# Leaf slots with dealt blocks, in place of every leaf's units, in the tree networks of a two-layer Perceiver kernel

## The chip, the cores and the metric

The kernel runs on one core of a Trainium2 chip. The metric is device time in microseconds of that core, as the median of the runs shown. The profile is one further execution of the same program, with its own time.

## The reference, cut to what matters

An input x of 16 batches of 64 tokens (1024 tokens in all, 256 features, float32) passes through two layers, each with a cross attention over 16 x 1601 memory rows, a second mixing step and a feed-forward part, each added to x. The change is in the last part of the second layer: three fast-feedforward networks f = q, k, v. Each is a binary tree of depth 4 with 15 nodes and 16 leaves, and each leaf is a small two-layer network of width 64. A token walks down the tree, and only its own leaf counts:

```python
def fff(x, node_w, node_b, w1, b1, w2, b2):          # for each of q, k, v
    cur = 0                                          # per token
    for _ in range(4):
        score = (x * node_w[cur]).sum(-1) + node_b[cur]
        cur = 2 * cur + 1 + (score >= 0)
    leaf = cur - 15
    sel = one_hot(leaf, 16)
    hidden = relu(einsum('nd,ldh->lnh', x, w1) + b1[:, None, :]) * sel.T[:, :, None]
    return einsum('lnh,lho->no', hidden, w2) + sel @ b2
# x = x + softmax(q k^T / 16) v, within each batch of 64 tokens, on x after a layer norm
```

The weights of one network are 1 MB for `w1` (256 x 1024: leaf l owns the columns 64 l to 64 l + 63), 1 MB for `w2` (1024 x 256) and 16 KB for `b2`.

## The kernel before, in words

**Order of the program.** First comes layer 0: cross attention with a top-32 choice, a retention step, self-attention, and a mixture of experts. The experts' tokens go through DRAM: an indirect DMA on POOL scatters rows to `disp` (L1025), SP reads them back (L1045), and another indirect DMA gathers the results (L1153). Then comes layer 1: the cross attention over the memory in 128 units (16 batches, 4 parts of the memory, 2 groups of heads), then for each half of the tokens (h = 0 and 1, 512 tokens each) the generator `after_attention(h)`: output projection, random features, a last layer norm, and the walk down the three trees. The networks come last.

**What sets the order.** In these stages the instructions of PE, DVE and ACT run in the order in which the code emits them (`tc.manual_schedule`), and Python generators written as steps are interleaved by hand. `LATE_STEPS` says how many steps of `after_attention(0)` run beside each of the last 16 attention units; what is left of it, and `after_attention(1)`, run beside the networks, one step at a time. The queues of SP and POOL are ordered by the framework's planner. Each engine and each queue is in order, so an instruction that waits holds up all behind it. A DMA issued by SP takes one of eight semaphores in turn, and it waits until the DMA that had that semaphore before it has landed.

**Steps of `after_attention(h)` that matter here.** SP reads the heads' results of half h from the DRAM tile `by_head` (L1397). `norm_steps` takes statistics on DVE and an inverse root and the scaling on POOL. `turned_half` turns tokens to features with PE transposes. `by_pairs` and `rates` are matmuls. The node scores are 8 small matmuls (L1482), and three rounds of five small DVE operations (L1505 to L1512) walk the trees; `cur` then holds the leaf of each token and network.

**The networks.** For each half h and network f there are three pieces of work. `hidden(i)` multiplies all 512 tokens by the whole `w1`: 8 blocks of 128 hidden units, two matmuls with 512 columns each (L1796), and ACT adds the bias and the relu (L1803). `leaves(i)` spreads the leaf numbers of the tokens over all partitions with PE (L1776). `masked(i, m)` sets the hidden units of other leaves to zero on DVE (L1785). `given(i)` multiplies by the whole `w2` (L1818 for q and k, L1830 for v) and adds `b2` of the leaf with a matmul of 16 partitions (L1823, L1836). All 16 leaves are thus computed for every token. `attended(h)` then does the 64 x 64 softmax attention (L1854 to L1883), and the rows go out by SP (L1888).

## Time and profile before

| what | us |
|---|---|
| median of 3 runs (lowest, highest) | 1532.55 (1529.1, 1533.01) |
| the profiled execution: its time | 1526.84 |
| the profiled execution: its span | 1525.1 |
| from the first hidden matmul of the networks to the end of the span | 231.8 (1293.3 to 1525.1) |
| PE busy in the windows 1293 to 1411 and 1411 to 1525.1 | 111.78 of 118, 106.78 of 114.1 |

The span runs from the first to the last instruction of the profiled execution. A float32 matmul appears as two records (a transpose as one), so 64 records are 32 matmuls. The mean duration of a group is that of one record with its latency; the pace of back-to-back matmuls is read from the chain or the timeline, where a matmul with 512 columns takes 0.86 us.

### The profile page before, as it was taken

What the parts mean: (1) busy time and instruction counts of PE and PEld (TensorE: products, weight loads), DVE (VectorE), ACT (ScalarE), POOL (GpSimd) and SP (SyncE); (2) the same over time, 40 slices, a digit from 0 to 9 for tenths busy, and PEclk for the clock granted to TensorE, in tenths of its full rate; (3) what the DMA queues carried; (4) which work ended last, traced back from release to release, by engine and by line L of the source; (5) the groups of instructions that cost most, each with busy time, mean ns of one, the idle gap of its engine ahead of it and who ended that gap; (6) DMA issues with size and microseconds to landing.
All of it is one profiled execution on the core that took longest, in us unless ns stands there. A gap on an engine that the chain in (4) does not pass through costs nothing.

```text
span 1525.1 us, 28151 instructions
## 1 busy us (share of the span) xinstructions
PE 1460.4 (96%) x10994; PEld 996.7 (65%) x10994; DVE 998.8 (65%) x2135; ACT 786.2 (52%) x1979; POOL 321.9 (21%) x789
## 2 busy tenths in 40 slices
PE   7999888999988999999999999999999998989999
PEld 4666546677866777777777777777777765446445
DVE  2888848771159877877787787778776666523332
ACT  4666422351056666666666666666666555211221
POOL 2000017202032223132312312230331322321000
PEclk9999999999989999999999999999999999999999
DMA  9455042034821011011001101110110121000000
GB/s 327 141 173 172 2 135 72 1 111 145 263 78 44 3 45 46 4 46 45 22 28 45 46 3 46 45 46 3 45 44 4 45 85 31 16 0 0 0 14 14
DMA packets 76597, 92.86 MB, mean 61 GB/s; under 512 B 2584, under 2 KB 71760, under 8 KB 76336
## 3 DMA queue, kind: packets, MB, share of 16 engines
q1 hardware_dynamic: 72912, 82.82, 17.0%
q0 software_dynamic: 2400, 7.20, 1.9%
q8 instruction: 86, 1.41, 0.4%
q10 hardware_dynamic: 1152, 1.05, 0.2%
q14 instruction: 47, 0.39, 0.1%
HBM read 85.82 MB, written 5.24 MB: 60 GB/s over the span
## 4 chain that ended last, share of the span: by engine, by line
PE 87%; DVE 7%; DMA 2%; ACT 1%; issue 1%; POOL 1%; DVEq 0%; POOLq 0%; SPq 0%; ACTq 0%
PE ps_v L624 12%; PE ps_k L602 11%; PE pt L1565 9%; PE sc L1530 7%; PE po L1585 7%; PE ps_h L1796 5%; PE ps_o L1818 4%; PE pt L325 3%; PE sc L338 3%; PE ps_p L209 3%; DVE nmax L1543 3%; PE pu L410 3%; PE pt L581 3%; PE ps_h L1069 2%; PE ps_v L1830 2%; PE ps_y L1083 2%
## 5 line engine op out<-in xcount | busy, mean ns | idle before, releaser
L1551 ACT ACTIVATE a<-sc,nmax 128x384 f32<-128x384 f32 (+2 forms) x512 | 304.4, 600 | 162.4 <-DVE nmax L1543 162.4
L1543 DVE TENSOR_REDUCE nmax<-sc 128x1 f32<-128x384 f32 (+2 forms) x512 | 258.1, 566 | 96.1 <-PE sc L1530 96.0
L1565 PEld LDWEIGHTS pt<-ident,a 128*128 128x128 f32 (+1 forms) x1664 | 188.2, 141 | 47.0 <-issue 26.4
L1573 DVE COPY aT<-pt 128x512 f32<-128x512 f32 (+1 forms) x288 | 191.2, 685 | 34.3 <-PE pt L1565 26.1
L602 PE MATMUL ps_k<-mT,w_x 128*128 128x384 f32 (+2 forms) x512 | 205.2, 524 | 1.1 <-ACT mT L586 1.1
L624 PE MATMUL ps_v<-w_x,mT 128*128 128x256 f32 (+1 forms) x832 | 202.7, 383 | 2.9 <-ACT kT L610 1.0
L1565 PE MATMUL pt<-ident,a 128*128 128x128 f32 (+1 forms) x1664 | 203.3, 273 | 0.0
L624 PEld LDWEIGHTS ps_v<-w_x,mT 128*128 128x128 f32 (+1 forms) x832 | 146.4, 187 | 25.3 <-DVE aT L1573 5.1
L602 PEld LDWEIGHTS ps_k<-mT,w_x 128*128 128x128 f32 x512 | 87.1, 189 | 104.6 <-issue 72.1
L1530 PE MATMUL sc<-kT,qh 32*128 32x384 f32 (+2 forms) x1024 | 124.0, 547 | 0.0
L1585 PE MATMUL po<-aT,v 128*32 128x128 f32 (+1 forms) x3328 | 118.3, 277 | 6.0 <-DVE aT L1573 6.0
L586 ACT ACTIVATE mT<-pt,cols 128x384 f32<-128x384 f32 (+2 forms) x128 | 86.7, 683 | 66.1 <-PE pt L581 65.9
L568 POOL TENSOR_SCALAR memt<-memt,m_nmean,m_rstd 128x256 f32<-128x256 f32 (+1 forms) x208 | 111.8, 554 | 1.8
L1551 ACT ACTIVATION_READ_ACCUMULATOR a<-sc,nmax 128x1 f32 x512 | 105.9, 207 | 0.0
L1585 PEld LDWEIGHTS po<-aT,v 128*32 128x32 f32 (+1 forms) x3328 | 82.6, 110 | 31.6 <-issue 14.4
L610 ACT ACTIVATE kT<-ps_k,cols 128x384 f32<-128x384 f32 (+2 forms) x128 | 76.0, 594 | 39.6 <-PE ps_k L602 39.6
L632 DVE COPY v<-ps_v 128x512 f32<-128x512 f32 (+1 forms) x112 | 64.9, 580 | 35.3 <-PE po L1585 28.0
L562 DVE BATCH_NORM_STATS2 m_st<-memt 128x6 f32<-128x256 f32 (+1 forms) x208 | 82.9, 403 | 5.8 <-DMA memt<-in_mem_dram 5.5
L1570 ACT COPY aT<-pt 128x512 f32<-128x512 f32 x128 | 75.6, 591 | 0.7 <-PE pt L1565 0.7
L1785 DVE SCALAR_TENSOR_TENSOR hT<-leafb,memt,hT 128x512 f32<-128x512 f32 x48 | 35.2, 746 | 60.0 <-ACT hT L1803 60.0
L581 PE MATMUL pt<-ident,memt 128*128 128x128 f32 (+1 forms) x416 | 67.4, 276 | 3.8 <-ACT mT L586 3.3
L1803 ACT ACTIVATE hT<-ps_h,cols 128x512 f32<-128x512 f32 x48 | 33.0, 687 | 73.4 <-PE ps_h L1796 73.4
(365 smaller groups left out, 2019.9 us busy)
## 6 DMA issues: line engine op xcount, KB each, us to landing
memt<-in_mem_dram SPq DMA_DIRECT2D x32, 1536.0 KB
w<-in_moe_w_dram SPq DMA_DIRECT2D x16, 1024.0 KB
memt<-in_mem_dram SPq DMA_DIRECT2D x32, 65.0 KB
w_x<-in_w_x_dram POOLq DMA_DIRECT2D x2, 1024.0 KB, 10.5
mT<-in_fff_w_dram SPq DMA_DIRECT2D x2, 1024.0 KB
kT<-in_fff_w_dram SPq DMA_DIRECT2D x2, 1024.0 KB
rows<-in_rows_dram SPq DMA_DIRECT2D x1, 1430.5 KB
X<-in_x_dram SPq DMA_DIRECT2D x2, 512.0 KB
```

Source lines behind the costliest of these rows:

```text
L562: nc.vector.bn_stats(out=st[0:m, c, :], in_=mt[0:m, c, :])
L568: nc.gpsimd.tensor_scalar(mt[0:m, c, :], mt[0:m, c, :], nmean[0:m, c : c + 1], rstd[0:m, c : c + 1], ALU.add, ALU.mult,)
L581: nc.tensor.transpose(pt[:, j * P : j * P + chunk(c)], mt[0 : chunk(c), c, dc * P : (dc + 1) * P], ident[0 : chunk(c), 0 : chunk(c)],)
L586: nc.scalar.activation(mT[:, dc, c0 * P : c0 * P + n], pt[:, 0:n], AF.Identity, bias=col("L1_norm_b", dc), scale=col("L1_norm_w", dc),)
L602: nc.tensor.matmul(ps[:, 0:n], lhsT=wk[:, dc, oc * P : (oc + 1) * P], rhs=mT[:, dc, n0 : n0 + n], start=(dc == 0), stop=(dc == 1),)
L624: nc.tensor.matmul(ps[0 : chunk(c), j, :], lhsT=mT[:, dc, c * P : c * P + chunk(c)], rhs=wv[:, dc, :], start=(dc == 0), stop=(dc == 1),)
L1530: nc.tensor.matmul(scs[j][:, 0:n], lhsT=qh[rs, oc, b, :, :], rhs=kT[rs, oc, c0 * P : c0 * P + n], start=True, stop=True,)
L1543: nc.vector.reduce_max(out=nm, in_=sc[:, 0:n], axis=AX.X, negate=True)
L1551: nc.scalar.activation(aj[:, 0:n], sc[:, 0:n], AF.Exp, bias=nm, accum_out=tot[:, blk, part : part + 1])
L1565: nc.tensor.transpose(pt[0:m, j * P : (j + 1) * P], a[j][:, c * P : c * P + m], ident)
L1573: nc.vector.tensor_copy(aT[0:m, :], pt[0:m, :])
L1585: nc.tensor.matmul(po[32 * j : 32 * j + 32, :], lhsT=v[0:m, c0 + c, blk * 32 : (blk + 1) * 32], rhs=aTs[c][0:m, j * P : (j + 1) * P], star ...
```

## The change

Tokens are sorted to slots by leaf, so that each token meets only its own leaf's weights.

1. For each half and network there is a DRAM tile `slots_in` of 1536 rows: 16 leaves with 64 slots each, and 8 further blocks of 64 slots for leaves with more than 64 tokens. `zeros()` clears all six (1.5 MB each) from SP during the attention.
2. `placed(h, leaf, xn)`, at the end of `after_attention(h)`, computes the slot of every token (a count of earlier tokens of the same leaf with matmuls on PE, and 22 small DVE operations), which leaf each of the 8 further blocks is dealt to, and scatters the rows of `xn` with 12 indirect DMAs on POOL.
3. The networks of a half run as nine thirds `third(h, f, c)` of 512 slots. c = 0 and 1 are the leaves 0 to 7 and 8 to 15 with their weights in place; c = 2 is the eight dealt blocks. `fetch_third`, two thirds ahead, reads the slots from DRAM and the biases `b2`. For c = 2 SP loads eight leaf numbers to registers and issues 24 DMAs (8 blocks, each with a piece of `w1`, of `w2` and of `b2`) whose source address is the register.
4. A third is 8 transposes, 16 matmuls 128 x 64 x 64, relu, 8 matmuls 64 x 64 x 256, an addition to the biases on DVE, and a 512 KB store to `slots_out`. After c = 2 four indirect DMAs on POOL gather the tokens' rows back; q and k are then turned again with 8 transposes.
5. `LATE_STEPS` is changed so that all of `after_attention(0)`, `placed` included, runs within the attention; `pause` counts in `after_attention(1)` are raised; and the networks of half 0 run beside `after_attention(1)`, those of half 1 after it. `hidden`, `leaves`, `masked` and `given` are gone.

```diff
-LATE_STEPS = {0: 1, 2: 2, 3: 2, 4: 1, 5: 1, 6: 2, 8: 1, 9: 1, 10: 1, 11: 1, 12: 2, 14: 1, 15: 1}
+LATE_STEPS = {0: 3, 1: 2, 2: 1, 3: 3, 5: 1, 6: 2, 7: 3, 9: 1, 10: 2, 11: 3, 12: 1, 13: 2}
+    def zeros():
+        zero = spare_rows[:, 512:768]
+        nc.vector.memset(zero, 0.0)
+        for h in range(2):
+            for f in range(3):
+                nc.sync.dma_start(
+                    out=slots_in[h][f].rearrange("(n p) d -> p n d", p=P),
+                    in_=zero.unsqueeze(1).to_broadcast([P, NSLOT // P, D]))
...
+    def placed(h, leaf, xn):
...
+        for f in range(3):
+            sent = scattered[h, f] = []
+            for k in range(4):
+                sent.append(nc.gpsimd.indirect_dma_start(
+                    out=slots_in[h][f],
+                    out_offset=bass.IndirectOffsetOnAxis(
+                        ap=to_rows[h][:, 3 * k + f : 3 * k + f + 1], axis=0),
+                    in_=xn[:, k, :], in_offset=None).ins)
...
+        def fetch_third(h, f, c):
+            xs = arrived[h, f, c] = work.tile([P, 4, D], F32, name="xs", tag="xs", bufs=3)
+            read = nc.sync.dma_start(out=xs, in_=slots_in[h][f][c * 512 : (c + 1) * 512, :]...)
...
+            y = filled[h, f, c] = places[(h + 3 * f + c) % 4]
+            if c < 2:
+                biases = fff_b2[f].rearrange("(m s) o -> s m o", s=2)
+                for side in range(2):
+                    nc.sync.dma_start(out=y[side * 64 : (side + 1) * 64, :, :],
+                        in_=biases[side, c * 4 : (c + 1) * 4, :].partition_broadcast(64))
+                return
+            _, numbers = nc.values_load_multi_w_load_instructions(
+                over_leaf[h][0:1, f * 8 : (f + 1) * 8], engines=[mybir.EngineType.SP], ...)
...
+            at = (h + f) % 2
+            for i in range(8):
+                one = bass.ds(numbers[i], 1)
+                sl = slice(i % 2 * 64, (i % 2 + 1) * 64)
+                nc.sync.dma_start(out=dealt1[at][:, i, :]..., in_=first[:, :, one, :]...)
+                nc.sync.dma_start(out=dealt2[at][sl, i // 2, :], in_=second[one, :, :]...)
+                nc.sync.dma_start(out=y[sl, i // 2, :], in_=fff_b2[f][one, :].to_broadcast([64, D]))
...
+        def networks(h):
+            thirds = [(h, f, c) for f in range(3) for c in range(3)]
+            for i, (_, f, c) in enumerate(thirds):
+                if i + 2 < len(thirds):
+                    fetch_third(*thirds[i + 2])
+                yield from third(h, f, c)
+                if c == 2:
+                    back(h, f)
+                if c == 1 and f > 0:
+                    turned_back(h, f - 1)
+                    yield
+            yield from attended(h)
...
         with tc.manual_schedule(engines=order):
-            for step, _ in enumerate(networks()):
...
+            for c in range(2):
+                fetch_third(0, 0, c)
+            work_of = networks(0)
+            for _ in joining:
+                next(work_of)
...
+            for _ in after_attention(1):
+                next(work_of, None)
+            for c in range(2):
+                fetch_third(1, 0, c)
+            run(work_of)
+            run(networks(1))
```

The new function that does the work of one third, with what is left out marked:

```python
        def third(h, f, c):
            xs = arrived.pop((h, f, c))
            xsT = work.tile([P, 2, 512], F32, name="xsT", tag="xsT")
            for dc in range(2):
                ...                                   # 4 transposes, copied by ACT (dc 0) or DVE (dc 1)
            yield
            ps = ps_f.tile([P, 4, WIDTH], F32, name="ps_h", tag="mm")
            ...                                       # 16 matmuls: 64 slots x 64 units, two halves of 128 features
            hT = row(("L1_bq", "L1_bv")[(f + c) % 2]).rearrange("p (j t) -> p j t", j=4)
            ...                                       # bias and relu: ACT for c < 2, DVE and ACT for c = 2
            yield
            y = filled.pop((h, f, c))
            for j0 in (0, 2):
                ps = ps_f.tile([P, 2, D], F32, name="ps_y", tag="mm")
                ...                                   # 4 matmuls: 64 slots x 256 outputs, one leaf each
                part = y[:, j0 : j0 + 2, :]
                nc.vector.tensor_tensor(part, ps, part, ALU.add)
            nc.sync.dma_start(
                out=slots_out[h][f][c * 512 : (c + 1) * 512, :].rearrange("(m p) d -> p m d", p=P),
                in_=y,
            )
            yield
```

## The prediction

> **What bounds the kernel now.** I read the page's busy shares and chain first, then busy time by stage, then the groups of the last stage, and last the rows nearest to what the change adds.
>
> ```profile
> PE 1460.4 (96%) x10994; PEld 996.7 (65%) x10994; DVE 998.8 (65%) x2135; ACT 786.2 (52%) x1979; POOL 321.9 (21%) x789
> PE 87%; DVE 7%; DMA 2%; ACT 1%; issue 1%; POOL 1%; DVEq 0%; POOLq 0%; SPq 0%; ACTq 0%
> ```
>
> PE is busy 96% and carries 87% of the chain that ended last. By stage (span; then busy time of PE, PEld, DVE, ACT, POOL; granted clock, DMA share, GB/s):
>
> ```profile
> 1250.00:1293.00 43.00, 37.15 (x396) 25.44 (x400) 27.98 (x63) 23.43 (x73) 9.62 (x28) 1.00 0.13 37
> 1293.00:1411.00 118.00, 111.78 (x361) 58.77 (x356) 44.98 (x118) 25.24 (x40) 28.69 (x67) 0.99 0.02 6
> 1411.00:1525.10 114.10, 106.78 (x373) 56.31 (x372) 31.60 (x58) 22.89 (x37) 0.00 (x0) 1.00 0.03 10
> ```
>
> The networks (from 1293) are PE's alone, with idle DMA queues. In the end of the attention PE already loses 6 of 43 us. The nearest rows to the new work (timeline: start, duration, records, idle before; and rows by tile):
>
> ```profile
> 1444.45 1.20 PE L1854 MATMUL ps_s<-kT,qT 128*64 128x64 f32 x32
> 194.56 5.83 PE L410 MATMUL pu<-memt,aT 128*64 128x256 f32 x52
> 352.80 0.97 POOL L1025 DMA_INDIRECT disp<-y,to_row  x1 [0.30 <-issue]
> 355.47 0.92 SPq L1045 DMA_DIRECT2D dsp<-disp  x2
> 359.46 1.94 PE L191 MATMUL ps_t<-ident,dsp 128*128 128x128 f32 x8 [3.38 <-DMA dsp<-disp]
> 360.00:365.00 5.00, 5.00 (x23) 4.71 (x22) 1.38 (x2) 1.17 (x2) 0.00 (x0) 0.50 0.02 7
> DMA to landing us min/median/max: 2.7/2.8/3.3
> 64.14 0.37 SPq L241 DMA_DIRECT2D memt<-in_mem_dram  x1
> 64.55 0.78 SPq L244 DMA_DIRECT2D memt<-in_mem_dram  x1
> L1505 DVE TENSOR_TENSOR rows<-memt,rows 128x180 f32<-128x180 f32 x6 | 2.1, 345 | 0.2
> L1349 DVE BATCH_NORM_STATS2 c_st<-X 128x6 f32<-128x256 f32 x8 | 3.3, 407 | 0.0
> ```
>
> From the last scatter of `disp` to its first use on PE is 359.46 - 352.80 = 6.7 us. SP issues a DMA in 0.37 to 0.46 us, one of 65 rows in 0.78. A scatter's or gather's landing takes 2.4 to 2.8 us.
>
> **The change part by part.**
>
> *Removed, on PE's path.* By the chain's paces: 96 matmuls of `hidden` x 0.86 = 82.5; 64 of `given` q, k x 0.86 = 55; 64 of v x 0.43 = 27.5; bias matmuls 8 x 1.05 + 8 x 0.62 = 13.4; `leaves` 24 x 0.33 = 8. Sum 186 us of the 231.8. The masks (48 x 0.75 = 36 us on DVE) lay beside it.
>
> *Added on PE.* A third: 8 transposes 0.9; 16 matmuls of the shape of L1854, 1.13; 8 matmuls at the pace of L410 (52 records, 5.7 us: 0.22 per matmul), 1.75. So 3.8 us, 18 thirds 68 us: PE is relieved of some 115 us. That is not the gain, since the rest becomes chain.
>
> *One third alone.* Transposes 0.9, copy 0.7, hidden 1.1, relu 0.3, outputs 1.75: PE can start the next after 4.8 us (c < 2). For c = 2 DVE's bias (2 x 0.35) and one relu (0.4) come between: about 6. Three thirds: 15.7 us.
>
> *What paces a network: the 24 register DMAs.* The order of SP's queue shows it: the store of third (f, 2), which waits for DVE, then the read of the slots of (f+1, 2), the register load, 24 DMAs, and only then the store of (f+1, 0). So the dealt weights of a network are fetched only after the c = 2 third of the one before, although their buffer is free. Loop: store and read issue 0.9; register load 1.3; 22 DMAs up to the last piece of `w1`; landing 2.2; then the rest of the third: last hidden matmuls, bias, relu, outputs, additions, 4.2 at full clock. No row shows a register-addressed DMA, nor one of 64 partitions: nearest are 0.42 (128 partitions, whole) and 0.78 (65 rows). With the register arithmetic I take 0.6: 13.4. The ends, 0.45 and 0.9, give 10 and 20. The loads' 8 registers are bounded by 0.6 (the floor in DMA: Bandwidth & Descriptors, Latency and other measured facts) and 2. Sum 22 us, against 15.7 us of thirds, which it covers.
>
> *Two rules that speak against it.* First the clock: after the idle 3.4 us at 356 the row has a granted clock of 0.50, and 8 transposes took 1.94 where 8 others at 340 took 1.07. TensorE: Matmul & The Clock Gate (Part 1) says that a window of about 3.4 us without work halves the clock and that as much sustained work restores it; its Part 4 adds that transposes don't count as work. PE has some 10 us idle in each loop. By the row the 1.8 us of outputs behind the wait double: 22 becomes 24 us, which I take. By the rule all thirds stay cold (3.8 becomes 7.6): the first two still hide behind the DMAs, and the loop is 24 to 26. Second, DMA: Bandwidth & Descriptors (Anatomy of one DMA, a software-queue fit) gives a DMA 2.0 us plus bytes over 436 KB/us: 2.15 for 64 KB. One after the other, 24 would take 52 us and the change would lose 140 us. But SP's waits let eight be in flight, and the trace shows issues 0.42 apart: three rounds of 2.2 to 3 us fit within 13.4.
>
> *Bytes.* A network moves 1.5 MB of slots, 1.5 of stores, 1 of biases, 1.5 dealt, 1 of scatter and gather: 6.5 MB, 20 us at the 340 GB/s of the start. Below the loop, so hidden, but it would bind at 20. `zeros` is 9.4 MB (28 us) in a stretch with 35 to 56 GB/s, behind the load of batch 5; the next load is 50 us later: nothing. Without that gap the batch's norm would wait up to 28 us. Six transposing loads of `b1` (3072 elements of 4 bytes, no row like them) stand behind half 0's `by_head` read, 80 us before the first use: nothing[...].
>
> *End of the attention.* The tree of half 0 (5.3 us of DVE from L1505 and its four like) and `placed` (22 DVE operations, 4 of them wide: 6 us; PE 2.5) now lie there, where DVE is busy 28 of 43 us and PE waits for it. Of 13.8 I take 9 (3 to 20): the end moves from 1293 to 1302. The 12 scatters (12 x 1.27) lie behind that on POOL, off the path, since SP reads the slots last.
>
> *Half 0.* Slots on PE at 1304.5 (issue after the last scores, 3.8 to use). `by_head` of half 1 is now read behind the dealt DMAs (issue about 1314.5, landed 1318), and DVE's statistics wait for it with all behind them. End of network q, E0: 1318 + 1.1 statistics + 0.7 copy + 1.1 + 5 = 1326. k: 1350, v: 1374. The output projection, features and norms of half 1 (some 20 us of PE) stand in the waits of these loops; if the dealt pieces came sooner they would be exposed.
>
> *Then, uncovered.* After v: store landed 1377; 4 gathers (5 us on POOL), behind which the last norm's 15 small POOL operations (4.3) and scaling (2.2) are queued: 1389. Turned 1.7, nodes 2, tree 5.3, `placed` 7: rows known at 1405. Register load, first DMAs; 4 scatters to 1408.8, and 6.7 to use. Dealt pieces of q: SP is held by the slots' read until 1411.2; then 1.3 + 7 x 1.6 + 2.2: 1425. Rest of the third 5.9: 1431. k 1455, v 1479. Store 3, gathers 3.8 + 2.8, weighted sum 1.1, last output 2.6 (before, DVE's last addition ended at 1522.5 and the span at 1525.1): 1492.
>
> *Sum.* Span 1525 - 33 = 1492, time 1494 against 1526.84. The median of before is 5.7 above that execution: **1500 us**.
>
> **The rivals.**
>
> *A: as above, a loop of 18 to 29 us.* The end moves by 5 loops' worth: 18.5 gives 1472, 29 gives 1525 less a little. For: SP's order is in the program. Against: the issue time is an estimate.
>
> *B: the queue costs more and the kernel gets slower.* Same place, SP's 24 DMAs per network: at 0.85 us each (near the 65-row row), or with eight in flight landing only after 7 us, the loop is 30 and the gain is gone; at 1.05 it is 35 and the time 1555. It decides at 0.85 us per DMA. For: shapes with 64 partitions and a register have no row. Against: that row may hold a full queue (1.5 MB just before).
>
> *C: the dealt pieces hide.* If an issue takes 0.4 and bytes flow, the loop falls to the thirds' 15.7: 1500 - 5 x 8.3 = 1458. Against: bytes alone need about 20.
>
> *D: the attention pays.* If the moved DVE work costs 30 us there instead of 9 (each DVE wait stops the units' softmax, and the scatters precede the last `by_head` write on POOL): 1521. For: PE waits for DVE at the end already. Against: POOL is idle enough (9.6 of 43).
>
> *E: slots don't thin the work.* The work is fixed by 24 blocks whatever the tokens, so that holds.
>
> **How the numbers follow.** A 0.54, B 0.28, C 0.08, D 0.10. About 0.3% (4.6 us) is what a measurement here can tell from no change. A is faster but for its slow end (0.04 same); D is 0.05 faster, 0.02 same, 0.03 slower; B is slower but for 0.02 same. Faster 0.50 + 0.05 + 0.08 = 0.63, same 0.08, slower 0.29. Range 1460 to 1560: C's end to B's 35 us loop. A alone: 1472 to 1525.
>
> **What would show it.** Right: PE busy about 30% in the last 200 us, a granted clock below 1 there; SP issuing without a break for 12 to 16 us per network; hidden matmuls of c = 2 waiting for the `w1` pieces by 5 to 10 us; dealt-to-dealt distance 22 to 26; the attention's end near 1302; rows of half 1 known near 1405. Wrong: issues of 0.4 with PE busy throughout (C), of 0.85 and more or waits of SP on its own DMAs (B), an attention end past 1315 (D), or slots landing far later than 6.7 us after the scatter.

## The result: 1569.55 us against 1532.78, slower by 2.4%

| | before | changed |
|---|---|---|
| median (runs) | 1532.78 us (4; 1529.1 to 1537.38) | 1569.55 us (4; 1566.71 to 1571.35) |
| ratio, 95% interval | 1 | 1.0237 [1.0205, 1.0269] |
| span of the profiled execution | 1525.1 us | 1568.3 us (its time 1570.01) |

The forecast was 1500 us, faster. The page of the changed kernel gives PE's busy time, and under the chain the share of each engine in it:

```profile
PE 1404.1 (90%) x11558; PEld 988.5 (63%) x11558; DVE 1001.0 (64%) x2161; ACT 773.6 (49%) x1996; POOL 368.1 (23%) x847
issue 3%; SPq 2%; DMA 1%; PE 1%; DVE 0%; another core or an unknown queue 0%; POOL 0%; ACT 0%; POOLq 0%; DVEq 0%; ACTq 0%
```

PE lost 56 us of busy time (1460.4 to 1404.1) and its share fell to 90%. The new chain breaks off after a few per cent, at a wait whose releaser the page cannot name, so the reading has to go by stage: the span of each window, then busy time of PE, PEld, DVE, ACT and POOL, granted clock, DMA share, GB/s.

```profile
1250.00:1293.00 43.00, 33.52 (x348) 23.09 (x346) 29.76 (x70) 18.91 (x56) 9.72 (x27) 0.96 0.34 100
1293.00:1335.00 42.00, 21.37 (x218) 15.16 (x218) 17.44 (x50) 13.20 (x43) 12.18 (x14) 0.76 0.26 88
1335.00:1428.00 93.00, 65.14 (x581) 44.50 (x582) 28.77 (x58) 18.11 (x46) 28.16 (x55) 0.82 0.66 183
1428.00:1472.00 44.00, 18.49 (x108) 14.79 (x107) 16.28 (x60) 1.90 (x4) 17.35 (x32) 0.61 0.33 99
1472.00:1568.30 96.30, 62.86 (x564) 40.65 (x564) 25.41 (x42) 14.95 (x42) 14.86 (x16) 0.73 0.64 185
```

The rows are: the last attention units, then their end (1293 is where the attention ended before), the networks of half 0, the stretch with no network, the networks of half 1 with the tail. In none is an engine full: after 1293 PE is busy 168 of 275 us (before, 219 of 232), at a granted clock of 0.61 to 0.82. The kernel now waits. Against the forecast's own steps:

| step | forecast | measured | excess |
|---|---|---|---|
| end of the attention | 1302 | 1332.7 | 30.7 |
| first slots of half 0 to the end of network q | 21.5 | 30.1 | 8.6 |
| to the ends of k and v | 24, 24 | 26.7, 36.0 | 14.7 |
| to the first slots of half 1 | 41.5 | 44.1 | 2.6 |
| to the end of network q | 15.5 | 24.4 | 8.9 |
| to the ends of k and v | 24, 24 | 26.3, 30.8 | 9.1 |
| to the end of the span | 13 | 14.9 | 1.9 |

An end of a network is the issue of its last store by SP. The excess is 76 us: 41 in the networks, 31 in the attention, 4.5 in the rest. Two places of PE's timeline show what kind of waits these are (start, duration, records, idle before it and releaser). The end of the attention:

```profile
1296.32 0.77 PE L1597 MATMUL ps_c<-ones,rows 128*48 128x1 f32 x8 [7.03 <-DVE rows L1590]
...
1304.24 0.66 PE L1735 MATMUL pt<-ident,a 128*128 128x128 f32 x4 [1.60 <-DVE aT L1743]
1306.02 0.22 PE L1614 MATMUL ps_c<-rows 48*48 48x1 f32 x2 [1.12 <-DVE rows L1612]
...
1307.18 0.21 PE L1641 MATMUL ps_c<-rows,ones 48*1 48x24 f32 x2 [0.60 <-DVE rows L1631]
...
1324.93 0.66 PE L1755 MATMUL po<-aT,v 128*32 128x128 f32 x8 [8.68 <-DVE aT L1743]
1327.64 1.08 PE L1755 MATMUL po<-aT,v 128*32 128x128 f32 x16 [2.05 <-ACT aT L1740]
```

The first four are the tree walk and `placed` in DVE's and PE's order: 10.4 us. The last two are a stop of 10.7 us while POOL issued the twelve scatters (1309.6 to 1324.6). The other place is the third behind the gathers of network k, in half 0:

```profile
1402.69 1.95 PE L2038 MATMUL ps_y<-kT,rows 64*64 64x256 f32 x16 [0.47 <-ACT rows L2019]
1407.05 0.47 PE L1423 MATMUL pt<-ident,w_x 128*128 128x128 f32 x1 [2.42 <-DMA w_x<-slots_out,to_row]
...
1410.98 1.33 PE L1423 MATMUL pt<-ident,w_x 128*128 128x128 f32 x5 [0.89 <-DMA w_x<-slots_out,to_row]
1412.11 3.62 PE L1467 MATMUL pf<-v,memt 128*128 128x512 f32 x4
...
1418.80 1.88 PE L1467 MATMUL pf<-v,memt 128*128 128x512 f32 x4
...
1422.32 1.15 PE L2006 MATMUL ps_h<-xsT,wide 128*64 128x64 f32 x32
```

PE stands at the transposes of what came back (`turned_back`), and the last third of network v is queued behind them. Its hidden matmuls come at 1422.3, after 9 us of random-feature matmuls of half 1 (L1467, L1472), the first four of them at about half pace, that stood in the same queue.

### The profile page after: what moved, and what is told of

The parts are those of the page before. It is cut to its first block, busy times and chain, and to the rows that moved or that the text cites. A ratio compares the mean times of both kernels' runs of the same rounds, so it can differ in the third digit from the quotient of the medians.

```text
span 1568.3 us, 30084 instructions
## 1 busy us (share of the span) xinstructions
PE 1404.1 (90%) x11558; PEld 988.5 (63%) x11558; DVE 1001.0 (64%) x2161; ACT 773.6 (49%) x1996; POOL 368.1 (23%) x847
## 5 line engine op out<-in xcount | busy, mean ns | idle before, releaser
L1755 PEld LDWEIGHTS po<-aT,v 128*32 128x32 f32 (+1 forms) x3328 | 84.0, 111 | 43.4 <-issue 21.7
L636 DVE COPY v<-ps_v 128x512 f32<-128x512 f32 (+1 forms) x112 | 64.9, 579 | 35.0 <-PE po L1755 26.3
L334 ACT COPY mT<-pt 128x512 f32<-128x512 f32 (+1 forms) x128 | 53.0, 524 | 20.7 <-PE pt L329 20.7
L585 PEld LDWEIGHTS pt<-ident,memt 128*128 128x128 f32 (+1 forms) x416 | 52.1, 143 | 17.5 <-ACT mT L590 4.2
```

The source lines that it names most:

```text
L585: nc.tensor.transpose(pt[:, j * P : j * P + chunk(c)], mt[0 : chunk(c), c, dc * P : (dc + 1) * P], ident[0 : chunk(c), 0 : chunk(c)],)
L1755: nc.tensor.matmul(po[32 * j : 32 * j + 32, :], lhsT=v[0:m, c0 + c, blk * 32 : (blk + 1) * 32], rhs=aTs[c][0:m, j * P : (j + 1) * P], star ...
```

## The experiments

The kernels were timed in five groups, each on one chip with the kernel before beside it: static_deal, turn_late, old_pace and scatter_late; after_again, static_turn, short_pauses and turn_bias_mm; mix2, mix2_old and mix2_early; after_third, wt_dve, mix and mix_old; turn_bias_old, tbo_act and tbo_pool. Between groups, ratios are compared. Only static_deal and static_turn leave a part of the computation out: the dealt blocks get the weights and biases of the blocks 0 to 7. "The networks" below is the time from the first slot transposes to the last store, both halves added, in the one profiled execution of each kernel: 174.3 us in the first profile, 133 in the forecast. The changed kernel's three profiles give 168 to 174, so a difference of 6 us between two such sums may be chance.

### The changed kernel again: after_again, after_third

> The changed kernel, unaltered. In its first profile the parts ahead of the networks, which no other kernel of this study alters up to 1240 us, ran 6 us later than in the profiles of the kernels with static blocks and with late transposes (first weighing of the attention at 469.4 us against 460.6 and 463.5), and PE stood 8.7 and 2.1 us at 1316 to 1327 where those show no such stop. Theory R (both belong to this program as it is built): 1566 to 1571 again, with the late start and the stop in the profile. Theory V (they vary from execution to execution, and the first profile caught both): a profile without the stop, and a time of 1555 to 1566.

> The changed kernel, unaltered, as the anchor for the other kernels of this comparison. It has measured 1569.5 and 1555.2 us on two occasions. In the first one, and in the kernels with all biases by product (1561.3 and 1562.7), PE stood 11 us at the end of the attention while POOL issued the twelve scatters, with DVE and ACT waiting for what the profile calls remote; in the second, and in six other kernels, it stood only 5.6 us, for ACT, which waited for a POOL operation behind the scatters. Theory R (the longer stop belongs to an occasion, not to a kernel): it shows here in this kernel if it shows in the next one and the one after, and the time is then 1563 to 1571, otherwise 1552 to 1558.

Measured: after_again 1555.2 us, ratio 1.0175 [1.0141, 1.0209]; after_third 1568.0 us, 1.0235 [1.0217, 1.0252]. The kernel is slower each time, by 26 or by 35 us. In after_again the networks took 168.1 us and the attention ended at 1323.7; the late start stayed (first weighing at 467.6), the stop of 10.7 us did not, so neither theory held whole. A shorter stop remained. In it PE stood for ACT, ACT for POOL, and POOL was behind its scatters (timelines of POOL, ACT and PE):

```profile
1320.46 0.96 POOL L1662 DMA_INDIRECT slots_in<-memt,to_row  x1 [0.30 <-issue]
1321.45 0.25 POOL L1772 TENSOR_TENSOR wt<-low,nmax 128x32 f32<-128x32 f32 x1
1321.73 0.23 ACT L1773 ACTIVATE wt<-wt 128x32 f32<-128x32 f32 x1 [6.89 <-POOL wt L1772]
1322.17 1.57 PE L1755 MATMUL po<-aT,v 128*32 128x128 f32 x24 [5.63 <-ACT pos L1762]
```

A 0.25 us operation of the last batch's softmax weights (`collect`) waits for twelve scatters of 1.27 us, ACT's copies wait behind it, and PE behind those. In after_third the same units show this on DVE and PE:

```profile
1315.92 0.49 DVE L1713 TENSOR_REDUCE nmax<-sc 128x1 f32<-128x321 f32 x1 [6.16 <-remote]
...
1319.47 0.49 DVE L1713 TENSOR_REDUCE nmax<-sc 128x1 f32<-128x321 f32 x1 [2.34 <-remote]
1323.97 1.51 PE L1755 MATMUL po<-aT,v 128*32 128x128 f32 x24 [11.49 <-DVE low L1770]
```

DVE waits for scores whose matmuls PE's records end by 1311, and the profile puts it down to "remote", a release that it can't place. The first profile, after_third, and all later kernels of this study but mix2_old show "remote" waits in the parts that the change made or moved; none of the eight profiles on the two chips of static_deal and after_again shows one, nor does that of the kernel before. So some 9 us of the first result (by the ratios, 1.0237 against 1.0175; 14 by the medians) go with the occasion and its chip, as theory R of after_third says. The chip alone does not decide it, since mix2_old shows none on the chip of mix2. What makes these waits was not found.

### What holds the networks: static_deal, turn_late, static_turn

```diff
# static_deal, static_turn: fixed addresses, 6 transfers for 24
+for cc in range(2):
+    nc.sync.dma_start(out=dealt1[at][:, :, cc * WIDTH : (cc + 1) * WIDTH], in_=first[:, cc, 0:8, :])
...                                   # and two transfers for w2, two for b2
# turn_late, static_turn
-if c == 1 and f > 0:
+if (f, c) in ((1, 2), (2, 2)):
     turned_back(h, f - 1)
```

> This kernel leaves part of the computation out: the third group of eight slot blocks of every network takes the weights and biases of the blocks 0 to 7 instead of the dealt ones, so tokens over a full block get a wrong network. Per network the 24 transfers with a register address and the one register load are replaced by 6 transfers with fixed addresses that carry the same bytes into the same tiles. Theory P (SP's issuing of the dealt transfers paces each network: 24 x 0.65 + 1.9 of register load = 17.5 us of SP, beside 6 us of its other issues): the loops from the end of one network to the end of the next fall from 26.7, 36.0, 26.3 and 30.8 us to about 18 to 20, the first network of each half gains 8 to 10, and the time falls from 1569.5 by 40 to 55, to 1515 to 1530. Theory L (the thirds are bound by their own chain of PE, ACT and DVE at a low granted clock, 5.4 to 9 us each): loops stay at 24 or more and the time is 1550 or more.

> The transposes of what came back from one network (q, then k) go behind the third third of the next network instead of behind its second; nothing is left out. In the changed kernel PE waited at them for the gathers of k from 1404.6 to 1412 with the last third of the value network queued behind. Theory G (PE's order at the gathers makes the loop of the value network 36 us in half 0 and 30.8 in half 1): the loop of half 0 falls by 5 to 8 us, that of half 1 by 1 to 4, and the time is 1558 to 1564. Theory P (SP's dealt transfers for the value network land at 1416.5 in any case): the loop falls by at most 5 and the time is 1564 to 1570.

> Static blocks (which leaves the dealt blocks' own weights and biases out, as before) together with the late transposes. With static blocks alone the loops stayed at 24 to 36 us although SP had hardly anything to issue. Theory G (what held them then was PE's order at the transposes of what came back: store, 5 us of issuing gathers, landing, 15.6 us in all from one network's last store to the transposes): the loops fall to 16 to 18 us and the time to 1505 to 1518. Theory L (a third's own chain of PE, ACT and DVE takes 8 us whatever is moved): the loops stay at 23 to 25 and the time is 1530 to 1541.

| kernel | ratio | networks, half 0 + half 1 |
|---|---|---|
| changed (after_again) | 1.0175 | 90.9 + 77.2 = 168.1 |
| turn_late (1551.1 us) | 1.0142 [1.0126, 1.0159] | 87.8 + 79.6 = 167.4 |
| static_deal (1541.0 us) | 1.0074 [1.0049, 1.0098] | 88.3 + 72.3 = 160.6 |
| static_turn (1508.4 us) | 0.9854 [0.9818, 0.9891] | 70.9 + 57.4 = 128.3 |

Alone the one gave the networks 0.7 us and the other 7.5; together they gave 39.8. The single gains are hardly more than two profiles of one kernel can differ by; scatter_late below, in effect the changed kernel on the chip of the two, took 172.8 and would make them 5 and 12. By the ratios of the medians the three gains are 5, 15 and 49 us, so in every reading both together bring more than twice the sum of the two. Neither theory P nor L of static_deal was right (L's loops of 24 us and more came, but not for its reason), and theory G of static_turn was, in half 1: two waits lay side by side, and each hid what the other's removal would have brought. Turn_late itself fell between its theories, with a loop of 31.4 us for v in half 0, where the changed kernel had 33.8 and 36.0. With static blocks PE stands at the gathers (static_deal, half 1):

```profile
1479.93 1.94 PE L2033 MATMUL ps_y<-kT,rows 64*64 64x256 f32 x16 [0.47 <-ACT rows L2014]
1484.40 0.42 PE L1423 MATMUL pt<-ident,memt 128*128 128x128 f32 x1 [2.27 <-DMA memt<-slots_out,to_row]
...
1486.53 1.33 PE L1423 MATMUL pt<-ident,memt 128*128 128x128 f32 x5 [0.85 <-DMA memt<-slots_out,to_row]
1487.65 1.91 PE L1990 MATMUL pt<-ident,xs 128*128 128x128 f32 x8
```

The store that ended network q was issued at 1472.0, so its rows are back on PE 12 to 15 us later. With late transposes PE stands at the dealt pieces instead. SP's timeline in turn_late (half 1, network k; each line is one issue):

```profile
1473.10 0.37 SPq L2050 DMA_DIRECT2D slots_out<-kT  x1
1473.52 1.69 SPq L1944 DMA_DIRECT2D xs<-slots_in  x1
1475.99 0.38 SPq L1975 DMA_DIRECT2D wide<-in_fff_w_dram  x1
...
1491.82 0.47 SPq L1983 DMA_DIRECT2D v<-in_fff_b_dram  x1
1492.48 0.44 SPq L1975 DMA_DIRECT2D wide<-in_fff_w_dram  x1
...
1501.56 1.10 SPq L2050 DMA_DIRECT2D slots_out<-v  x1
```

and PE's beside it (five waits for pieces of `w1`, 7.3 us in all; three of them left out):

```profile
1484.80 0.45 PE L2006 MATMUL ps_h<-xsT,wide 128*64 128x64 f32 x6 [0.22 <-DVE xsT L1998]
1487.49 0.45 PE L2006 MATMUL ps_h<-xsT,wide 128*64 128x64 f32 x6 [2.25 <-DMA wide<-in_fff_w_dram]
...
1494.63 0.69 PE L2006 MATMUL ps_h<-xsT,wide 128*64 128x64 f32 x6 [1.55 <-DMA wide<-in_fff_w_dram]
1496.85 3.68 PE L2038 MATMUL ps_y<-wide,rows 64*64 64x256 f32 x16 [1.53 <-ACT rows L2030]
```

This is the forecast's loop, and its terms can be read off: store, read and register load 2.9 us (1473.10 to 1475.99), 22 issues 16.9 (to the end of the last piece of `w1` at 1492.9), landing 1.7 (to 1494.63), rest 6.9 (to the store at 1501.56): 28.4. Within the 16.9 us SP waited only 1.5 for transfers of its own to land, so it is the issuing that takes the time. The waits halve PE's clock on the way: the granted clock is 1.00 from 1472 to 1484.8, 0.64 over the waits to 1496.8 and 0.50 behind them, and the output matmuls take 3.68 us where those of the two thirds before took 1.94. With both waits gone networks k and v of half 1 take 17 to 18 us, three thirds by their own chain (static_turn, network k; in half 0, beside the steps of half 1, they take 21 and 23, and the first networks 28 and 22):

```profile
1466.44 1.09 PE L1990 MATMUL pt<-ident,xs 128*128 128x128 f32 x8
...
1471.75 1.09 PE L1990 MATMUL pt<-ident,xs 128*128 128x128 f32 x8
...
1478.20 1.09 PE L1423 MATMUL pt<-ident,memt 128*128 128x128 f32 x8
```

A third with its weights in place takes 5.3 us, the dealt one 6.5.

### A third of the dealt transfers without leaving work out: turn_bias_mm

```diff
-nc.sync.dma_start(out=y[sl, i // 2, :], in_=fff_b2[f][one, :].to_broadcast([64, D]))
+for i in range(2 * j0, 2 * j0 + 4):          # in the third, c == 2; then an ACT copy to y
+    nc.tensor.matmul(pb[i % 2 * 64 : (i % 2 + 1) * 64, i // 2 - j0, :],
+        lhsT=over_has[h][:, f, i : i + 1].to_broadcast([48, 64]),
+        rhs=home["V0"][0:48, 3072:3328], start=True, stop=True)
```

> Late transposes, and the biases of the dealt blocks come from a product of the leaf marks with the bias rows (8 small matmuls of 48 rows and 2 copies by ACT a network) in place of 8 of the 24 transfers with a register address; nothing is left out. To be compared with the late transposes alone (1551.1 us). Theory P (SP's order of issue paces the networks wherever the gathers do not): 8 x 0.65 = 5.2 us a network less on SP, the loops of 26.8, 31.4, 28.5 and 29.9 us each fall by 4 to 5, and the time is 1526 to 1535. Theory L (the thirds' own chain paces them): PE gets 8 more matmuls and ACT two more copies in the third that ends each network, 2 to 3 us on the chain, and the time is 1552 to 1566.

Measured: 1528.3 us, ratio 0.9991 [0.998, 1.0002]; the networks 76.1 + 68.8 = 144.9 us against 167.4 with late transposes alone. Theory P: 22.5 us over six networks, 3.7 each, for 8 issues a network, where 8 x 0.65 = 5.2 had been put. It is level with the kernel before, and no kernel of this study with the whole computation was faster.

### The stretch between the halves: short_pauses

The edit is the pause counts alone.

> In the steps after attention of half 1 the pauses (steps in which only the networks of half 0 go on) are cut from 3, 5, 1, 5, 2, 1, 5, 1 to 3, 3, 0, 3, 0, 0, 3, 0; nothing is left out. Theory C (the 44 us between the last store of half 0 and the first slot transposes of half 1 are the rest of half 1's chain, which could have run beside the networks of half 0): the stretch falls to 20 to 30 us, and the time by 10 to 20, to 1550 to 1560. Theory W (PE takes its work in order, and so stands at each norm of half 1 with the slots of half 0 queued behind): the networks of half 0 lengthen by what the stretch loses, and the time is 1564 to 1575.

Measured: 1538.4 us, ratio 1.0061 [1.0039, 1.0082]. Theory C: from the last store of half 0 (1406.5) to the first slots of half 1 (1437.9) it is 31.4 us against 43.4 in after_again, which is near its 20 to 30, and the networks took no longer (85.2 + 80.5 us). The two long waits of PE in it:

```profile
1414.52 2.05 PE L2110 MATMUL ps_f<-v,amid 128*128 128x256 f32 x4 [5.18 <-DMA v<-slots_out,to_row]
...
1437.90 1.97 PE L1995 MATMUL pt<-ident,xs 128*128 128x128 f32 x8 [13.13 <-DMA xs<-slots_in]
```

The stretch is now the gathers of v and the scatters, with their landing; the norms have moved under the networks.

### The end of the attention: old_pace, scatter_late, wt_dve

```diff
# old_pace
-LATE_STEPS = {0: 3, 1: 2, 2: 1, 3: 3, 5: 1, 6: 2, 7: 3, 9: 1, 10: 2, 11: 3, 12: 1, 13: 2}
+LATE_STEPS = {0: 1, 2: 2, 3: 2, 4: 1, 5: 1, 6: 2, 8: 1, 9: 1, 10: 1, 11: 1, 12: 2, 14: 1, 15: 1}
...
+run(late)                 # behind the last attention unit
# wt_dve, in collect
-nc.gpsimd.tensor_tensor(wt, low.unsqueeze(2).to_broadcast(wide), nmax, ALU.subtract)
+eng = nc.gpsimd if places is None else nc.vector
+eng.tensor_tensor(wt, low.unsqueeze(2).to_broadcast(wide), nmax, ALU.subtract)
```

> The order of the late steps inside the last two memories' units is that of the kernel before; what is then left of half 0 (three tree levels, the places, the scatters) is run after the last attention unit. Nothing is left out. Theory D (the 30 us by which the attention ended later than forecast are the tree walk and the places, which stand in DVE's and PE's queues between attention units): the attention ends at 1293 to 1298, as before; the walk (10 us), the places (10 to 14 us with their waits between PE and DVE) and the scatters (15 us) then run uncovered, the first transposes come at 1335 to 1342, and the time is 1570 to 1577: about the same, since the cost is only moved. Theory E (something else in the attention part has grown, such as the pace of DMA issue or code): the attention ends after 1310 and the time is 1585 or more.

> The twelve scatters of half 0 on POOL (and the four small operations behind them) are issued after the last attention unit instead of inside the unit before it; nothing is left out. In the changed kernel PE stood still for 8.7 and 2.1 us at 1316.3 to 1327.6 while POOL issued these scatters (1309.6 to 1324.6), with DVE and ACT waiting for something that the profile cannot name. Theory S (the scatters hold up the attention): that stall goes, the attention ends 10 to 11 us earlier (1322 against 1332.7), the scatters then run uncovered from about 1322 to 1338, and the first slot transposes come at about 1342 against 1335: the time is 1575 to 1580. Theory T (the stall has another cause, such as instructions that arrive late): the stall stays where it is, the attention ends at 1330 to 1333, and the time is 1583 to 1590.

> The two small weight operations of the last memory's collection (difference and product, 128 x 32) run on DVE instead of POOL, where they stood behind the twelve scatters of half 0 (16 us); nothing is left out. ACT waited 6.9 us for the first of them, with the last copies of the attention behind it and PE behind those for 5.6 us. Theory Q (the scatters hold the end of the attention through this operation): that wait goes, the attention ends 5 to 6 us earlier; the first slot transposes then wait for the scatters themselves, which end on POOL as late as before, so the time is 0 to 3 us under the changed kernel's. Theory S (the scatters hold up DVE and ACT in another way): the stop stays at 5 us or more and the time is the same.

old_pace: 1548.6 us, 1.0122 [1.0105, 1.0139]. The attention ended at 1298.0, as before, against 1323.7, and yet the first slots came at 1321.4 against 1323.7. Theory D as to the place (theory E, 1310 or later, fell): the walk, the places and the scatters are one chain of 23 us that ends at nearly the same time inside the attention or behind it. By the ratios it is 8 us faster than the changed kernel, where that theory said about the same, with the first slots at 1335 to 1342; 2.3 of them are the earlier slots, and the rest was not followed.

scatter_late: 1557.5 us, 1.0179 [1.0162, 1.0196]. POOL's order is the planner's, and it put the scatters where they had been (first at 1304.4, the attention's end at 1322.8), so the edit tested nothing and theories S and T stay open.

wt_dve: 1566.8 us, 1.0227 [1.0208, 1.0245], with after_third on one chip. PE stood 11.47 us as in after_third (11.49), for "remote" waits. On such a chip POOL's operation is hidden by the longer stop, so the wait seen in after_again could not be taken away here; that it is a cause there rests on its row alone.

### Adding up: mix2, mix2_old, mix2_early, mix, mix_old

mix2 is late transposes, short pauses, and all biases by product, also those of the blocks in place (with `ident` as marks). mix has only the dealt ones by product. The ending "old" adds the edit of old_pace; "early" sets the steps {0: 3, 1: 2, 2: 1, 3: 3, 5: 3, 6: 3, 8: 2, 9: 2, 10: 2, 11: 2, 12: 1}.

> Late transposes, short pauses, and the biases of all slot blocks (not only the dealt ones) from products with the bias rows: a network's issues on SP fall from 34 transfers (24 with a register address) to 22 (16). Nothing is left out. Taken one by one against the changed kernel of the same chip (1555.2 us) late transposes gave 4 us, dealt biases by product 23 more, short pauses 17. Theory A (two bounds, SP's order and PE's order at the gathers, must both be moved, and the stretch between the halves is a third, separate one): the gains add, 1555 - 4 - 23 - 17 = 1511, and the four bias broadcasts that also leave SP (2 to 5 us a network on it) bring 1500 to 1508. Theory B (with SP free the chain of a third is the bound, and the added products and copies lie on it; the norms of half 1 now stand in PE's order between shorter thirds): 1515 to 1525.

> As mix2, and the late steps of half 0 at the pace of the kernel before, with the rest after the last attention unit. Alone that pace gave 6.6 us (1548.6 against 1555.2) although the first slot transposes came at 1321.4 against 1323.7. Theory D (the tree walk and the places cost the same inside the attention as behind it): within 3 us of 2 us faster than mix2. Theory U (behind the attention PE, DVE and POOL have nothing else, and by_head of half 1, written earlier, lets half 1 start earlier): 6 to 10 us faster than mix2.

> As mix2, and the late steps of half 0 set one unit earlier from the second norm on, so that the places are known one attention unit (6 to 7 us) sooner. Theory C (half 0's chain of norms, walk, places and scatters ends after the attention and so sets when the first slots come): the first slot transposes come 3 to 7 us earlier and the time falls by 3 to 7 against mix2. Theory W (the norm on POOL takes longer than a unit and PE stands for what is gained): within 2 us of mix2.

> Late transposes, the dealt blocks' biases (and only these) by product, and short pauses: the three that gained by themselves, without the bias products of the static blocks, which put 2.5 us on every third (7.6 to 8.2 us from store to store against 5.3). Nothing is left out. Theory A (the gains add: -4, -23 and -17 against the changed kernel's 1555.2): 44 us below the changed kernel in this comparison, 1508 to 1516 where that is 1555. Theory B (with half 1's chain moved up beside shorter networks, PE stands at its norms): the short pauses give less than 8, and the time is 20 to 30 us below the changed kernel.

> As mix, with the late steps of half 0 at the pace of the kernel before and the rest behind the attention. Alone this gave 6.6 us, and with all biases by product 12 us where the longer stop showed. Theory D: the stop of the attention behind the scatters (5.6 us, or 11) goes while the chain of half 0 ends 2 us earlier, so 3 to 7 us under mix without the longer stop, 10 to 13 under it with it. Theory N (the two paces cost the same): within 2 us of mix.

| kernel | us | ratio |
|---|---|---|
| mix2 | 1561.3 | 1.0172 [1.0151, 1.0194] |
| mix2_old | 1549.2 | 1.0102 [1.008, 1.0125] |
| mix2_early | 1562.7 | 1.0186 [1.0164, 1.0209] |
| mix (chip of after_third, 1.0235) | 1543.1 | 1.0076 [1.0057, 1.0096] |
| mix_old (same chip) | 1534.9 | 1.0013 [1.0001, 1.0025] |

mix2 missed both its theories. Its thirds take 7.5 to 9.7 us from store to store (half 1: 1480.70, 1489.15, 1496.93). The products stand in PE's order between a third's hidden and output matmuls, and their copies in ACT's order ahead of the relu (mix2, half 1, a third with its weights in place; PE's lines, then ACT's):

```profile
1482.56 1.03 PE L2002 MATMUL ps_h<-xsT,memt 128*64 128x64 f32 x28 [0.37 <-DVE xsT L1994]
1483.53 1.94 PE L2016 MATMUL ps_b<-v,ident 48*64 48x256 f32 x16
1486.37 1.94 PE L2049 MATMUL ps_y<-mT,rows 64*64 64x256 f32 x16 [0.90 <-ACT rows L2030]
1485.52 0.58 ACT L2026 COPY v<-ps_b 128x512 f32<-128x512 f32 x1 [0.28 <-PE ps_b L2016]
1486.00 0.93 ACT L2030 ACTIVATE rows<-ps_h,cols 128x64 f32<-128x64 f32 x4
```

SP was relieved where it no longer mattered, and PE and ACT were loaded where they did. mix2_old is 12 us under mix2, more than either of its theories said. mix2_early brought its slots no earlier (1343.5 against 1336.2) and its time is the same (theory W). mix is 25 us under after_third, not 44 (nearer theory B): the stretch fell to 32.9 us, but network v of half 0 took 30.1 where turn_bias_mm had 24.7. mix_old took off another 8 us, as old_pace had (theory D). In it, with the scatters behind the attention, DVE's "remote" waits at the end of the attention (8.2 us in mix, on the same chip) are gone, so there the long stop goes with the scatters beside the last units.

### Is SP still the bound? turn_bias_old, tbo_act, tbo_pool

turn_bias_old is turn_bias_mm with the edit of old_pace. tbo_act issues the pieces of `w2` by `nc.scalar.dma_start`, four behind the relu of each of the first two thirds; tbo_pool by `nc.gpsimd.dma_start`.

> Late transposes, dealt biases by product, and the late steps of half 0 at the old pace with the rest behind the attention; the pauses stay as in the changed kernel. Nothing is left out. Late transposes with dealt biases stood level with the kernel before (ratio 0.9991), the old pace took off 6.6 us alone, 8.2 with the short pauses beside it. Theory A (the end of the attention is a separate cost): ratio 0.993 to 0.997 to the kernel before. Theory B (the 6 to 8 us come back in the networks): 0.998 to 1.003.

> As turn_bias_old, and the 8 transfers a network of the dealt second-layer weights are issued by ACT, four behind each of the first two thirds' activations, with a register load of its own on ACT. Nothing is left out. Theory P (SP's order of issue is still the bound: 16 dealt, 4 bias, 3 store and 3 read transfers and a register load a network): 8 x 0.65 = 5.2 us a network leave SP, the loops of 20 to 26 us fall by 3 to 5, and the time is 15 to 28 us under turn_bias_old. Theory L (ACT's issues and its wait for the register load stand between activations and copies that PE waits for): the time is the same or up to 12 us longer.

> As turn_bias_old, and the same 8 transfers are issued by POOL, whose direct transfers took 0.9 us each in this kernel's traces, with a register load of its own. Nothing is left out. Theory P: 15 to 28 us under turn_bias_old, as for ACT. Theory O (POOL's own order: the gathers of the network before wait for their store to land, the dealt transfers stand behind them or in front of them, 8 x 0.9 to 1.3 = 7 to 10 us): the time is the same or up to 20 us longer.

Measured on one chip, again one with "remote" waits: 1547.7, 1551.0 and 1546.6 us; ratios 1.0093 [1.0076, 1.011], 1.0122 [1.0103, 1.0142], 1.0094 [1.0079, 1.0108]. Theory P fell: the issues moved to ACT cost 3 us (theory L), those moved to POOL nothing. The waits of half 1's networks k and v in turn_bias_old (who waited for whom: us in total, times, longest) say why:

```profile
PE ps_y L2053 <- ACT rows L2034: 4.0, 4, 2.5
PE ps_h L2009 <- issue: 3.7, 4, 2.4
SPq L2065 <- DVE kT L2064: 14.9, 2, 8.6
```

PE no longer waits for a dealt piece, and SP itself waits 15 us for DVE's sums to store. What is left is the thirds' own chain and waits that the profile can't name. No ratio here is as low as turn_bias_mm's on its chip, so whether the old pace adds to it stays open.

## Why the prediction was wrong

**PE's relief was right in kind and half as large.** PE is no longer full: after 1335 us it is busy 63% (146.5 of 233.3 us), at a granted clock of 0.73 in half 1. But its busy time fell by 56 us, not by some 115, and the sign "about 30%" did not come: the eighteen thirds keep PE busy 99.6 us (transposes 23.5, hidden 27.8, outputs 48.3), not 68, since many run at half clock. The forecast said that the gain would be what the new waits left, and they left less than nothing.

**Slots to the end of a network: the step that failed is "what paces a network".** Its place was right (SP's 24 register-addressed transfers, PE waiting at the `w1` pieces), its sum was not. Term by term, in turn_late where nothing else covers it: store, read and load 2.9 us for 2.2; 22 issues 16.9 for 13.4 (13.2 by its own 0.6), that is 0.77 each (0.66 when SP runs free, 0.9 in the first half of the pass); landing 1.7 for 2.2; rest 6.9 for the cold 5.9. So 28.4 for 24, which is near rival B's deciding point (0.85 an issue, a loop of 30). B's other reading, transfers that land late with eight in flight, was not it: SP's waits for its own transfers are 1.5 us of the pass.

**A wait that was in no sum: the gathers in PE's order.** The forecast priced store, gathers and landing once, after v. But `turned_back(h, f - 1)` puts them in front of the last third of every network but the first, 15 us after the store. Static_turn shows that this and SP's issues together cost the networks 40 us, and either removed alone brought 8 or less (12, against scatter_late): a sum of single terms misses a second wait of about the same length. Beyond the two the forecast's 15.7 us for three thirds was good: 17 to 18 in half 1.

**End of the attention: 9 us for the moved work was too little, and "off the path" for the scatters was wrong.** The score matmuls of the attention, with their first and last start, in the kernel before, the changed kernel and old_pace:

```profile
L1530 PE MATMUL sc<-kT,qh x1024: 427/558/692, 452.8 to 1286.8; 32*128 32x384 f32 x85, 32*128 32x512 f32 x43, 32*128 32x321 f32 x43
L1700 PE MATMUL sc<-kT,qh x1024: 428/585/1217, 459.2 to 1314.4; 32*128 32x384 f32 x85, 32*128 32x512 f32 x43, 32*128 32x321 f32 x43
L1700 PE MATMUL sc<-kT,qh x1024: 428/559/692, 456.8 to 1291.0; 32*128 32x384 f32 x85, 32*128 32x512 f32 x43, 32*128 32x321 f32 x43
```

From first to last that is 834.0 us before, 855.2 changed (854.2 in after_again) and 834.2 in old_pace: the moved steps cost 21.2 us, where the forecast took 9 and allowed 20. PE's waits at the walk and the places are 10.4 of them; the rest was not divided. Behind the last scores the attention took 18.3 us where it took 8.0 before. That is the stop beside the scatters, which the forecast priced at nothing because SP reads the slots last. In after_again they held a small POOL operation of the softmax, and through ACT PE, for 5.6 us; in the first profile PE stood 10.7, for "remote" waits of DVE and ACT whose cause is open. The other 8 of the 31 are a start of the attention that is 6.4 us later (other profiles of this study start between 449.6 and 461.8, so it is not put down to the change) and 1.8 us by which the attention before ended after the 1293 that the forecast counted from. Rival D had the place, the size (30 us instead of 9) and both kinds of reason, DVE's waits and scatters in front of other work on POOL. The price would have been nearly the same elsewhere: in old_pace the attention pays nothing and the slots come no more than 2.3 us sooner.

**The uncovered stretch (41.5 forecast, 44.1) and the tail (13, 14.9)** were right in length; their parts were not compared one by one. That the stretch could be cut by 12 us with fewer pauses was not seen.

**The clock.** The row of 0.50 behind an idle engine was the right one: the matmuls behind a wait for pieces took 3.68 us for 1.94, and the eight transposes behind the 13 us wait for slots took 1.97 for 1.09. The other reading of the rule in the Trainium skill's TensorE: Matmul & The Clock Gate (Part 1, with Part 4), that all thirds stay cold, did not hold: in turn_late the outputs of the first two thirds of every network ran at 1.94, but for one behind the wait for slots. Where PE stood more often they were slow too: in half 1 of the first profile four of these six took 3.3 to 3.7.

**The result** lies with B's and D's costs together, about 41 and 31 us on a gain of 33 (6 of the 31 being the late start). They were weighed as separate cases, 0.28 and 0.10, each against a main case with the other at its low value; nothing in the range stood for both, and the range ended at 1560.

## What to carry to other kernels

When a change turns one full engine into a chain of round trips, list every wait in the loop and not only the longest: here the two longest were about equal, and taking out one brought the networks 1 to 8 us where both brought 40. Price what stands behind a burst on an in-order queue, however small: a 0.25 us operation behind fifteen microseconds of scatters stopped ACT and PE. And work that is taken off a queue has to land off the chain: the same bias products gained 22 us in one third of each network and lost 15 (mix2 against mix, by the ratios) in all three, where they lay between the matmuls of every third.

## What the hardware showed that was not expected

- A register-addressed transfer from SP mostly occupied it 0.38 to 0.53 us and came every 0.66 us when SP ran free; over a whole pass with slots, stores and other landings about, 0.77.
- The same program took 1555.2 us on one chip and 1568.0 on another, where the kernel before took 1529.0 and 1533.3. The profiles differ in waits that the profile puts down to "remote", in the end of the attention (11.5 us of PE) and at the relus of some thirds (19 us of ACT in all in after_third). What makes them stays open; the one profile of the kernel before, on neither of the two occasions, has none.
